# Keys and values of the first attention layer as seven products of quarters instead of eight blocks

## The chip, the cores and the metric

The kernel runs on one core of one Trainium2 chip. The metric is the device time of one execution in microseconds; lower is better. Four runs of the kernel before took 1992.8 to 1999.78 us, with a median of 1995.32 us. All arithmetic is in 32-bit floats.

## What is computed

Two layers follow one another on x, 32 sequences of 64 tokens with 512 features (2048 rows), each with cross attention to a context of the same shape and a feed-forward part:

```python
x = x + L0_xattn(_layernorm(x), ctx, Wq, bq, Wkv, bkv, Wo, bo)
x = x + L0_ffn(_layernorm(x), ...)
x = x + L1_xattn(_layernorm(x), ctx, ...)
x = x + L1_ffn(_layernorm(x), ...)
```

The change lies in the first line, whose core is

```python
q = (query @ Wq + bq).reshape(B, L, NKV, G, HDIM)       # 8 groups of 4 heads of 128
k_, v_ = jnp.split(kv @ Wkv + bkv, 2, axis=-1)          # 8 key heads, 8 value heads
scores = jnp.einsum('blkgd,bmkd->bkglm', q, k) * scale  # within a sequence of 64
attn = jax.nn.softmax(scores, axis=-1)
o = jnp.einsum('bkglm,bmkd->blkgd', attn, v).reshape(B, L, NHEAD * HDIM)
return o @ Wo + bo
```

So for each of 8 groups there is one key head and one value head of 128 features, made from 512 context features for all 2048 rows, and shared by four query heads.

## The kernel before

The 2048 rows are cut into four chunks of 512 rows (eight sequences). Weights and activations lie in SBUF, products go to PSUM, and the language's scheduler orders the instructions of each engine by their dependences; matmuls that are wrapped in `pin` keep the order in which the program writes them. So the order of TensorE (PE) in this layer is written out by hand, and the orders of VectorE (DVE), ScalarE (ACT), GpSimd (POOL) and the DMA queue of SyncE (SP) follow from the scheduler.

**The order of the work.** `order` lists 32 pairs of a chunk c and a group g: the chunks 0 and 1 by turns for all eight groups, then the chunks 2 and 3. One pair is one iteration; two iterations with the same g are one visit, which shares the weights of that group. An iteration i does, in PE's order:

1. the transposes of the softmax result of iteration i-1 (`attn0_turn`, L554, tile pt_o),
2. the query products of iteration i (`attn0_queries`, tiles pqx, pqy, pqz, pqv), between them the mix of the values of iteration i-1 (`attn0_mix`, tile po) and the first of its output products (`attn0_out`, tiles ppx, ppy, ppz),
3. the scores of iteration i (`attn0_scores`, tile sc), 
4. the last three output products of iteration i-1,
5. the keys and values of iteration i+1 (`attn0_keys`, tile pk, and `attn0_values`, tile pv).

The softmax (L365 to L372: maximum, difference, exponential on ScalarE, sum, reciprocal, product) runs on DVE and ScalarE while PE does steps 4 and 5, and is wanted by step 1 of the next iteration.

**Keys and values before.** `attn0_keys` multiplies the weights (512 x 128) with the transposed context (512 x 512) in four matmuls of 512 columns, and ScalarE adds the bias on the way to SBUF (L469). `attn0_values` multiplies the other way round, so that tokens stand on the partitions: four blocks of 128 tokens, four matmuls of 128 columns each, then one DVE copy (L480). In the profile each matmul of 32-bit floats is two instructions, each with a weight load of its own (PEld).

**Strassen's scheme, already used.** The query and output products are made of quarters. Of both operands (512 x 512) the kernel forms sums of quarters: `left_sums` and `right_sums` (L398 to L401 and L408 to L411) are four additions or subtractions each, one of them in place. Seven products of quarters then give the result in place of eight (in Winograd's form, with partial sums that are shared). The products that are shared collect in one PSUM bank x: the first product is copied out by ScalarE (u1), the second is added to the same bank and copied again (u2), then the third (u3). The others go to banks y, z and v, and DVE adds the copies to them (`close`, L502). So PE must wait with the second product on x until the first copy has read it, and with the second product on z until DVE has read z. `quarter` (L426) issues one such product: four matmuls of 256 columns for a 256 x 256 quarter with a contraction of 256.

**Where the sums are made.** The sums of the rows of a chunk are made on DVE by `attn0_in` (with the normalisation L445 and transposes L452); those of the query weights by POOL in `open_visit`, at the end of each odd iteration; those of the output weights by POOL after the scores of each even iteration. POOL also adds the output bias to x (L448).

**Loads.** `load_attn0` loads the weights of a group into one of two slots of the tile `weights`: keys (L121), values (L123), queries (L124), output (L125). `load_ctx` (L186) loads a chunk of the transposed context into `ctx_q`. `clear_list` (L287) fills 4 MB of DRAM with zeros every four iterations; the scheduler places these early. All are issued on SP's queue, in order, each waiting for its place to be free.

**Buffers.** The pool `work` holds four tiles of 128 x 2048 (`t8`: queries and mixed values), three of 128 x 1024 (`t4`: probabilities and their transposes) and seven of 128 x 512 (`t2`: copies, keys, values, normalised rows). PSUM has eight banks: four `mm`, two `tr` (for the x of each scheme), two `sc`.

After the layer, `fold_latent` multiplies two weights of the feed-forward part (tiles pt_fc, pf) between the last output products, and `ffn_in` (L703 to L713) normalises and transposes the first chunk.

Of the kernel before, what the change touches and what calls it, by code (L numbers as in the profile page):

```python
# [12 lines left out]
ALU = mybir.AluOpType  # L13
# [16 lines left out]
def layers(ctx: ExitStack, tc: tile.TileContext, a: dict, out: bass.AP):  # L30
# [5 lines left out]
    xpool = ctx.enter_context(tc.tile_pool(name="xres", bufs=1))  # L36
    work = ctx.enter_context(tc.tile_pool(name="work", bufs=2))
    small = ctx.enter_context(tc.tile_pool(name="small", bufs=4))
    banks = ExitStack()
    pools = {"psum": banks.enter_context(tc.tile_pool(name="psum", bufs=2, space=PSUM))}  # L40
    dram = ctx.enter_context(tc.tile_pool(name="dram", bufs=1, space=bass.MemoryType.DRAM))


# [4 lines left out]
    def quarters(at, n):  # L48
# [3 lines left out]
    rows_q = [quarters(0, 7), quarters(3584, 7)]  # L52
    ctx_q = [
        cells[:, at : at + KT * CH].rearrange("p (k n) -> p k n", k=KT) for at in (7168, 9216)
    ]
    wq_sums, wo_sums, o_sums = (quarters(at, 3) for at in (11264, 12800, 14336))
# [14 lines left out]
    def t8(name):  # L71
        return work.tile([P, 4, 512], F32, tag="t8", name=name, bufs=4)

    def t4(name):
        return work.tile([P, 2, 512], F32, tag="t4", name=name, bufs=3)

    def t2(name):
        return work.tile([P, 512], F32, tag="t2", name=name, bufs=7)

# [18 lines left out]
    def pin(ins):  # L98
        return tc.keep_in_program_order(ins)
# [11 lines left out]
    def rows(ap):  # L111
        return ap.rearrange("(k p) n -> p k n", p=P)

    def part(w, at, k, n):
        return w[:, at : at + k * n].rearrange("p (k n) -> p k n", k=k)

    def load_attn0(g, slot, between=lambda: None):
        w = weights[:, slot]
        wq, wk = part(w, 0, KT, 512), part(w, 2048, KT, P)
        wv, wo = part(w, 2560, KT, P), part(w, 3072, 4, HID)  # L120
        nc.sync.dma_start(wk, rows(a["Wkv"][:, g * P : (g + 1) * P]))  # L121
        between()
        nc.sync.dma_start(wv, rows(a["Wkv"][:, (NG + g) * P : (NG + g + 1) * P]))  # L123
        nc.sync.dma_start(wq, rows(a["Wq"][:, g * 512 : (g + 1) * 512]))  # L124
        nc.sync.dma_start(wo, rows(a["Wo"][g * 512 : (g + 1) * 512, :]))  # L125
        return wq, wk, wv, wo

# [57 lines left out]
    def load_ctx(c, dst):  # L185
        nc.sync.dma_start(dst, rows(a["ctxT"][:, c * CH : (c + 1) * CH]))  # L186

    for c in range(NC):
        for i in range(c * TT, (c + 1) * TT):
            nc.sync.dma_start(xs[i], a["x"][i * P : (i + 1) * P, :])  # L190
        if c == 0:
            w_next = load_attn0(0, 0, between=lambda: load_ctx(0, ctx_q[0]))
        if c == 1:
            load_ctx(c, ctx_q[c])

# [199 lines left out]
    def left_sums(engine, a11, a12, a21, a22, sums):  # L395

        s1, s2, s4 = (sums[:, i] for i in range(3))
        engine.tensor_tensor(s1, a21, a22, ALU.add)  # L398
        engine.tensor_tensor(s2, s1, a11, ALU.subtract)
        engine.tensor_tensor(a21, a11, a21, ALU.subtract)  # L400
        engine.tensor_tensor(s4, a12, s2, ALU.subtract)  # L401
        return {"11": a11, "12": a12, "22": a22, "1": s1, "2": s2, "3": a21, "4": s4}
# [59 lines left out]

    def attn0_keys(g, c, w):
        n = f"a{g}_{c}"
        pk = ps_mm(f"pk_{n}")
        ct = ctx_q[c % 2]
        accumulate_next(pk, [(w[1][:, k, :], ct[:, k, :]) for k in range(KT)])
        kT = t2(f"kT_{n}")
        nc.scalar.activation(kT, pk, AF.Identity, bias=bkv[:, g : g + 1])  # L469
        return kT  # L470

    def attn0_values(g, c, w):
        n = f"a{g}_{c}"
        pv = ps_mm(f"pv_{n}")
        ct = ctx_q[c % 2]
        for t in range(TT):
            s = slice(t * P, (t + 1) * P)
            accumulate_next(pv[:, s], [(ct[:, k, s], w[2][:, k, :]) for k in range(KT)])
        v = t2(f"v_{n}")
        nc.vector.tensor_copy(v, pv)  # L480
        return v

# [51 lines left out]

    def attn0_scores(g, c, kT, qT):
        n = f"a{g}_{c}"
        at = t4(f"at_{n}")
        for p in range(2):
            sc = ps_sc(f"sc_{n}_{p}")
            for b in range(8):  # L540
                s = slice(b * 64, (b + 1) * 64)
                accumulate_next(sc[:, s], [(q_pair(qT, p, b), kT[:, s])])
            softmax(at[:, p, :], sc, 1.0 / math.sqrt(128), f"{n}_{p}")
        return at

    def attn0_turn(g, c, at):
        n = f"o{g}_{c}"

        atT = work.tile([P, TT, 2, P], F32, tag="t4", name=f"atT_{n}", bufs=3)
        for p in range(2):  # L550
            pt = ps_mm(f"pt_{n}_{p}").rearrange("p (t n) -> p t n", t=TT)
            for t in range(TT):
                pin(
                    nc.tensor.transpose(pt[:, t, :], at[:, p, t * P : (t + 1) * P], ident)  # L554
                )
            nc.scalar.copy(atT[:, :, p, :], pt)
        return atT

    def attn0_mix(g, c, v, atT):
        n = f"o{g}_{c}"  # L560

        oT = t8(f"oT_{n}").rearrange("p i (h n) -> p i h n", h=2)
# [55 lines left out]
    def open_visit(v):  # L618
# [3 lines left out]
        visits[v] = {"w": w, "q": left_sums(nc.gpsimd, k11, k21, k12, k22, wq_sums)}  # L622

    rights = {0: attn0_in(0)}
    open_visit(0)
    visits[0]["o"] = right_sums(nc.gpsimd, *w_quarters(visits[0]["w"][3]), wo_sums)
    w = visits[0]["w"]
    kT, v = attn0_keys(0, 0, w), attn0_values(0, 0, w)
    last = None
    for i in range(len(order) + 1):  # L630
        q = iter(())
# [4 lines left out]
        if last is not None:  # L636
            gl, cl, vl, atl = last
            atT = attn0_turn(gl, cl, atl)
        next(q, None), next(q, None)
        if last is not None:  # L640
            o = attn0_out(gl, cl, attn0_mix(gl, cl, vl, atT), visits[(i - 1) // 2]["o"])
        else:
            o = iter(())
# [6 lines left out]
        if i < len(order):  # L650
            at = attn0_scores(g, c, kT, qT)
            last = (g, c, v, at)
        else:
            fold_latent(latent)
# [4 lines left out]
        if i % 2 == 0:  # L659
            if i > 0:  # L660
                visit["o"] = right_sums(nc.gpsimd, *w_quarters(visit["w"][3]), wo_sums)
            if i // 2 + 1 < len(visits):
# [14 lines left out]
        if i + 1 < len(order):  # L677
            cn, gn = order[i + 1]
            if cn not in rights:
                rights[cn] = attn0_in(cn)  # L680
            w = visits[(i + 1) // 2]["w"]
            kT, v = attn0_keys(gn, cn, w), attn0_values(gn, cn, w)
            if gn == NG - 1 and cn + 2 < NC:
                load_ctx(cn + 2, ctx_q[cn % 2])
    down, fc2 = load_down()
# [4 lines left out]
    for c in range(2):  # L690
        load_ctx(c, ctxT[c])


# [862 lines left out]
```

## Time and profile before

| what | value |
|---|---|
| median of four runs | 1995.32 us (1992.8 to 1999.78) |
| profiled execution, whole | 1991.96 us |
| its span, first to last instruction | 1990.1 us |
| granted clock of PE, mean | 0.986 |
| first attention, about | 15 to 1242 us |
| one iteration of it | 37.80 us |
| loads of Wkv | 32 of 256 KB, 2.7 us from issue to landing |

The profile is one execution on the chip. In its groups a line names the place in the code, the engine, the operation, the tile written and the tiles read, the shape, the count, and after the bar the busy time in us, the mean duration of one in ns, and the idle time of the engine just before, with what ended it. PE is the matrix engine, PEld its weight loads, which run beside it; the ends of matmuls are modelled, so that neighbours in a stream overlap by some tenths of a microsecond, and their pitch is read from start to start. In a timeline a row is a start, a length, an engine, a line and an operation; neighbours of one kind are merged (x8).

### The profile page before, as it was taken

The page shows a single profiled execution, that of the slowest core. Times are in us where ns is not written, and L with a number is a line of the kernel's source. Part 1 is how long each engine was busy: PE and PEld are TensorE (multiplying, and loading weights), DVE is VectorE, ACT ScalarE, POOL GpSimd, SP SyncE. Part 2 cuts the span into 40 slices and gives each one's busy share as a digit, 9 for nine tenths or more (in the row PEclk, how much of TensorE's full clock was granted, in tenths as well). Part 3 has the DMA queues.
Part 4 walks back from the last instruction along what each step waited for, and adds up shares of the span by engine and source line. Part 5 has one row for each costly group of instructions (what it writes and reads, how often), then busy time and mean ns, then how long its engine had stood idle before and what let it go on. Part 6 is the DMA issues. An engine that isn't in the chain of part 4 may idle for free.

```text
span 1990.1 us, 26205 instructions
## 1 busy us (share of the span) xinstructions
PE 1908.9 (96%) x10492; PEld 1523.8 (77%) x10492; DVE 1020.6 (51%) x1999; ACT 487.2 (24%) x921; POOL 475.6 (24%) x501
## 2 busy tenths in 40 slices
PE   6999999999999999999999999999999999979993
PEld 5888888888888888888888888687778776655441
DVE  8445345344456644544534545455466466773515
ACT  1211211121121221121112112311221565542221
POOL 5120111111112111211211220141444535540105
PEclk9999999999999999999999999999999999989997
DMA  9993110100120110110100011100003201124628
GB/s 323 275 301 111 44 42 12 54 33 22 57 70 22 54 32 22 54 32 22 54 32 22 22 50 61 55 1 12 0 22 138 65 12 54 70 85 132 217 91 274
DMA packets 136087, 151.69 MB, mean 76 GB/s; under 512 B 4768, under 2 KB 88544, under 8 KB 135968
## 3 DMA queue, kind: packets, MB, share of 16 engines
q1 hardware_dynamic: 124960, 122.70, 19.6%
q0 software_dynamic: 5392, 17.11, 2.6%
q10 hardware_dynamic: 5616, 10.23, 1.4%
q8 instruction: 84, 1.38, 0.3%
q14 instruction: 35, 0.29, 0.1%
HBM read 92.60 MB, written 56.36 MB: 75 GB/s over the span
## 4 chain that ended last, share of the span: by engine, by line
PE 89%; DVE 6%; ACT 2%; DMA 2%; POOL 1%; issue 1%; POOLq 0%; SPq 0%; DVEq 0%; ACTq 0%
PE ppx_o L426 11%; PE pqx_a L426 8%; PE py L105 6%; PE sc_a L105 6%; PE pqz_a L426 6%; PE pv_a L105 6%; PE ppz_o L426 6%; PE pk_a L105 5%; PE po_o L105 3%; PE pdx_f L426 3%; PE ppy_o L426 3%; PE pp L105 3%; PE pqv_a L426 3%; PE pqy_a L426 3%; PE phx_f L426 2%; PE pq_b L105 1%
## 5 line engine op out<-in xcount | busy, mean ns | idle before, releaser
L408 POOL TENSOR_TENSOR arena<-weights 128x512 f32<-128x512 f32 x16 | 20.3, 1268 | 563.0 <-PE ppz_o L426 563.0
L367 ACT ACTIVATE at_a<-at_a 128x512 f32<-128x512 f32 x64 | 40.4, 631 | 444.0 <-DVE at_a L366 444.0
L105 PE MATMUL py<-arena,xT 128*128 x312 | 140.6, 593 | 0.2 <-ACT xT L1272 0.2
L105 PEld LDWEIGHTS pv_a<-weights,arena 128*128 128x128 f32 x1024 | 119.4, 192 | 15.3 <-issue 15.3
L426 PE MATMUL pqz_a<-arena 128*128 128x256 f32 x512 | 122.9, 383 | 4.8 <-DVE qT_a L502 4.8
L426 PE MATMUL ppx_o<-weights,oT_o 128*128 128x256 f32 x512 | 122.8, 383 | 0.1
L105 PEld LDWEIGHTS sc_a<-kT_a,qT_a 128*128 128x128 f32 x1024 | 120.0, 193 | 1.8
L426 PE MATMUL pqx_a<-arena,weights 128*128 128x256 f32 x512 | 121.1, 379 | 0.0
L495 ACT ACTIVATE u_a<-pqx_a,bq 128x256 f32<-128x256 f32 x192 | 80.5, 470 | 163.2 <-PE pqx_a L426 163.2
L105 PE MATMUL pv_a<-weights,arena 128*128 128x128 f32 x1024 | 119.5, 275 | 0.0
L105 PE MATMUL sc_a<-kT_a,qT_a 128*128 128x64 f32 x1024 | 118.3, 274 | 0.0
L105 PE MATMUL pk_a<-arena,weights 128*128 128x512 f32 x256 | 115.1, 592 | 0.0
L480 DVE COPY v_a<-pv_a 128x512 f32<-128x512 f32 x32 | 22.2, 692 | 178.0 <-PE pv_a L105 177.9
L426 PEld LDWEIGHTS pqz_a<-arena 128*128 128x128 f32 x512 | 98.4, 192 | 18.6 <-issue 5.1
L586 DVE TENSOR_TENSOR x<-ppx_o,x 128x512 f32<-128x512 f32 x128 | 86.9, 679 | 45.6 <-PE ppx_o L426 43.8
L426 PEld LDWEIGHTS ppx_o<-weights,oT_o 128*128 128x128 f32 x512 | 94.9, 190 | 11.9 <-ACT oT_o L576 0.5
L426 PEld LDWEIGHTS pqx_a<-arena,weights 128*128 128x128 f32 x512 | 94.9, 190 | 11.5
L502 DVE TENSOR_TENSOR qT_a<-pqz_a,u_a 128x512 f32<-128x512 f32 x64 | 44.2, 691 | 112.2 <-ACT u_a L495 80.2
L105 PEld LDWEIGHTS py<-arena,xT 128*128 128x128 f32 x312 | 56.2, 190 | 55.9 <-issue 55.3
L105 PEld LDWEIGHTS pk_a<-arena,weights 128*128 128x128 f32 x256 | 48.4, 190 | 47.3 <-issue 45.9
L398 POOL TENSOR_TENSOR arena<-weights 128x512 f32<-128x512 f32 x18 | 23.2, 1289 | 245.2 <-PE pqz_a L426 242.2
L502 DVE TENSOR_TENSOR qT_a<-pqy_a,u_a 128x512 f32<-128x512 f32 x32 | 22.1, 691 | 114.9 <-PE pqy_a L426 114.9
(368 smaller groups left out, 3826.1 us busy)
## 6 DMA issues: line engine op xcount, KB each, us to landing
xg<-zero SPq DMA_DIRECT2D x8, 4096.0 KB, 26.0
weights<-in_Wq SPq DMA_DIRECT2D x16, 1024.0 KB, 5.3
weights<-in_Wo SPq DMA_DIRECT2D x16, 1024.0 KB, 5.2
xr<-xg SPq DMA_DIRECT2D x39, 256.0 KB, 3.4
yg<-y ACTq DMA_DIRECT2D x39, 256.0 KB, 2.6
weights<-in_Wkv SPq DMA_DIRECT2D x32, 256.0 KB, 2.7
arena<-in_ctxT SPq DMA_DIRECT2D x8, 1024.0 KB, 5.2
arena<-in_W_e SPq DMA_DIRECT2D x8, 1024.0 KB, 6.2
```

What stands on the lines that cost most here:

```text
L105: nc.tensor.matmul(ps, lhsT, rhs, start=(i == 0), stop=(i == len(pairs) - 1))
L367: nc.scalar.activation(dst, dst, AF.Exp, scale=scale)
L398: engine.tensor_tensor(s1, a21, a22, ALU.add)
L408: engine.tensor_tensor(t1, b12, b11, ALU.subtract)
L426: nc.tensor.matmul(ps[:, m, :], left[:, k, m * P : (m + 1) * P], right[:, k, :], start=first and m == i == k == 0, stop=i == len(pairs) - ...
L480: nc.vector.tensor_copy(v, pv)
L495: nc.scalar.activation(u[:, m * 256 : (m + 1) * 256], ps[:, m * 256 : (m + 1) * 256], AF.Identity, bias=bq[:, 4 * g + 2 * heads + m : 4 * ...
L502: nc.vector.tensor_tensor(q5[:, heads, :, 4 * half : 4 * half + 4, :], ps.rearrange("p (m b q) -> p m b q", m=2, q=64), u.rearrange("p (m ...
L586: nc.vector.tensor_tensor(dst, ps.rearrange("p (m n) -> p m n", m=2), dst, ALU.add)
```

## The change

In the first attention, keys and values of two neighbouring groups in one chunk are now one product of a 512 x 256 weight with the 512 x 512 context, made of quarters by the seven products of the scheme above. A quarter of the weight is 256 x 128, so a product is two matmuls of 256 columns for keys and four of 128 columns for values. One call makes the keys, or the values, of two groups for one chunk; a period of four iterations has two calls for keys and two for values, one at the end of each iteration, where keys and values of the next iteration stood before. Keys are made half a period (two iterations) ahead of their pair of groups, values at the end of the iteration whose mix first uses them. The first call stands before the loop, two stand in the first iteration, and the last two iterations have none.

POOL makes the sums of quarters for the weights (`kv_left`) and for the context (`ctx_right`, once for each chunk). The weights are loaded for two groups at once, the keys into slot 0 and the values into slot 1 of `weights`; a chunk of the context comes in four loads of a quarter each. Keys and values lie in a tile of five places, given out in turn.

The layer gets a pool of its own, `work0`, with two tiles t8, two t4 and four t2, and with the room for the sums and for keys and values. It is closed after the layer, and the pool `work` with the former counts (4, 3, 7) is opened for the rest.

```diff
-    work = ctx.enter_context(tc.tile_pool(name="work", bufs=2))
+    room = ExitStack()
+    pools["work"] = room.enter_context(tc.tile_pool(name="work0", bufs=2))
+    bufs = {"t8": 2, "t4": 2, "t2": 4}
...
+    def load_kv(g, value):
+        w = part(weights[:, value], 2048, KT, 2 * P)
+        at = (value * NG + g) * P
+        nc.sync.dma_start(w, rows(a["Wkv"][:, at : at + 2 * P]))
+        return w
...
-    def attn0_keys(g, c, w):
...
-        accumulate_next(pk, [(w[1][:, k, :], ct[:, k, :]) for k in range(KT)])
...
-    def attn0_values(g, c, w):
...
+    kv_tiles = pools["work"].tile([P, 5, 512], F32, tag="kv", name="kv", bufs=1)
...
+    def kv_left(w, value):
+        k11, k12, k21, k22 = (
+            w[:, 2 * j : 2 * j + 2, i * P : (i + 1) * P] for i in range(2) for j in range(2)
+        )
+        return left_sums(nc.gpsimd, k11, k12, k21, k22, kv_sums[value])
+    def ctx_right(c):
+        x = ctx_q[c % 2]
+        return right_sums(nc.gpsimd, x[:, 0], x[:, 1], x[:, 2], x[:, 3], ctx_sums[c % 2])
+    def attn0_kv(value, g, c, left, right):
...
+        def product(ps, x, y, first=True):
+            x, y = left[x], right[y]
+            for m in range(2 if value else 1):
+                for k in range(2):
+                    sides = (y[:, k, m * P : (m + 1) * P], x[:, k, :]) if value else (
+                        x[:, k, :], y[:, k, :]
+                    )
...
+        def keep(ps, i, name):
+            u = t2(f"{name}_{n}")[:, 0:256]
+            if value:
+                nc.scalar.copy(u, ps[:, 0:256])
+            else:
+                nc.scalar.activation(
+                    u, ps[:, 0:256], AF.Identity, bias=bkv[:, g + i : g + i + 1]
+                )
+            return u
+        def close(i, half, ps, u):
+            nc.vector.tensor_tensor(
+                dst[i][:, half * 256 : half * 256 + 256], ps[:, 0:256], u, ALU.add
+            )
+        x = ps_tr(f"px_{n}")
+        product(x, "11", "11")
+        u1 = keep(x, 0, "u1")
+        y = ps_mm(f"py_{n}")
+        product(y, "12", "21")
+        close(0, 0, y, u1)
+        product(x, "2", "2", first=False)
+        u2 = keep(x, 0, "u2")
+        z = ps_mm(f"pz_{n}")
+        product(z, "1", "1")
+        product(x, "3", "3", first=False)
+        u3 = keep(x, 1, "u3")
+        close(1, 1, z, u3)
+        y = ps_mm(f"pw_{n}")
+        product(y, "22", "4")
+        close(1, 0, y, u3)
+        product(z, "4", "22", first=False)
+        close(0, 1, z, u2)
...
     rights = {0: attn0_in(0)}
+    kv_lefts = [kv_left(w_k, 0), None]
+    ctx_rights = {0: ctx_right(0)}
+    kv_lefts[1] = kv_left(w_v, 1)
     open_visit(0)
...
-    kT, v = attn0_keys(0, 0, w), attn0_values(0, 0, w)
+    make_kv(0, 0, 0)
...
-            kT, v = attn0_keys(gn, cn, w), attn0_values(gn, cn, w)
...
+        p, step = divmod(i, 4)
+        if i == 0:
+            ctx_rights[1] = ctx_right(1)
+            make_kv(0, 0, 1)
+        if step < 2:
+            make_kv(1, p, step)
+        elif p + 1 < NP:
+            make_kv(0, p + 1, step - 2)
+        cp, gp = kv_chunk(p, step % 2)
+        if step < 2 and gp == NG - 2 and cp + 2 < NC:
+            load_ctx(cp + 2, ctx_q[cp % 2])
+            ctx_rights[cp + 2] = ctx_right(cp + 2)
+        if step == 0 and p + 1 < NP:
+            kv_lefts[0] = kv_left(load_kv(kv_chunk(p + 1, 0)[1], 0), 0)
+        elif step == 1 and p + 1 < NP:
+            kv_lefts[1] = kv_left(load_kv(kv_chunk(p + 1, 0)[1], 1), 1)
...
+    room.close()
+    pools["work"] = ctx.enter_context(tc.tile_pool(name="work", bufs=2))
+    bufs.update({"t8": 4, "t4": 3, "t2": 7})
```

In the prediction the seven products of a call are named p1 to p7 in the order of `attn0_kv`.

## The prediction

> **What bounds the kernel now.** I read the page's first part, then the busy times by stretch, then the timeline of one iteration. The page:
>
> ```profile
> PE 1908.9 (96%) x10492; PEld 1523.8 (77%) x10492; DVE 1020.6 (51%) x1999; ACT 487.2 (24%) x921; POOL 475.6 (24%) x501
> ```
>
> Busy times by stretch (stretch, its length, then PE, PEld, DVE, ACT and POOL busy with instruction counts, granted clock, DMA share and GB/s), two neighbouring iterations of the first attention:
>
> ```profile
> 462.20:500.00 37.80, 37.80 (x210) 32.35 (x209) 17.53 (x29) 6.91 (x13) 3.76 (x3) 1.00 0.01 1
> 500.00:537.80 37.80, 37.80 (x210) 32.34 (x209) 17.53 (x29) 6.91 (x13) 6.29 (x5) 1.00 0.21 70
> ```
>
> PE never rests at full clock; every other engine is below half. So from about 50 to 1190 us time falls one for one with PE work, unless the new order makes PE wait. The timeline (start, length, engine, line, operation) shows what is replaced and when DVE is free there:
>
> ```profile
> 537.21 0.69 DVE L372 TENSOR_TENSOR at_a<-at_a,rs_a 128x512 f32<-128x512 f32 x1
> ...
> 537.76 3.60 PE L105 MATMUL pk_a<-arena,weights 128*128 128x512 f32 x8
> 537.96 0.69 DVE L586 TENSOR_TENSOR x<-ppx_o,x 128x512 f32<-128x512 f32 x1
> ...
> 541.19 3.73 PE L105 MATMUL pv_a<-weights,arena 128*128 128x128 f32 x32
> ...
> 544.76 0.49 PE L554 MATMUL pt_o<-ident,at_a 128*128 128x128 f32 x3
> ```
>
> From the first key matmul to the transposes is 544.76 - 537.76 = 7.00 us, 32 times in the layer. DVE has finished the softmax at 537.90 and its last old addition at 538.65.
>
> **1. PE work removed.** After: 32 calls, 16 for the keys and 16 for the values of two groups in a chunk, each seven products. A key product is two matmuls of 256 columns. The same shape stands in the query products: eight instructions 1.73 us apart (513.36 is a stalled one; 515.19 to 516.92), 0.216 each, two per matmul. So 4 x 0.216 = 0.865 us a product, 6.05 a call. A value product is four matmuls of 128 columns, eight instructions at 3.57/32 = 0.11 or, by the weight loads, 0.108: 0.87 to 0.89 us, 6.07 to 6.25 a call. Against 7.00 that saves 0.95 and about 0.90; I take 0.94 x 32 = **30.1 us**. Bounds 27 to 31.
>
> **2. Waits added inside a call.** Order on PE: p1 into x, p2 into y, p3 again into x, p4 into z, p5 into x, p6 into a new bank, p7 again into z. p3 and p5 need ScalarE to have copied x; p7 needs ScalarE's copy after p5 and then the DVE sum that reads z. Before, the same scheme in the queries had 1.73 us of cover a product and no such pause; here it is 0.865. The durations of shapes that exist:
>
> ```profile
> L495 ACT ACTIVATE u_a<-pqx_a,bq 128x256 f32<-128x256 f32 x192 | 80.5, 470 | 163.2 <-PE pqx_a L426 163.2
> ...
> L154 ACT COPY weights<-pf 128x256 f32<-128x256 f32 x4 | 1.5, 372 | 1.8 <-PE pf L96 1.8
> ...
> L1014 DVE TENSOR_TENSOR x<-pp,x 128x256 f32<-128x256 f32 x32 | 13.5, 423 | 66.6 <-PE pp L105 66.6
> ```
>
> Handovers, from the timeline: PE's shown end to ScalarE 0.04 (509.72 to 509.76), ScalarE to DVE 0.03 (519.69 to 519.72), either to PE's weight load 0.05 (1246.01 to 1246.07). A group's shown end is its last start plus 0.38; a group of eight that starts after a wait takes 2.00 instead of 1.89, so 0.11 more.
> - p3, p5 (keys): from the start of p1, its end is at 0.65 + 0.38 = 1.03, the copy ends at 1.03 + 0.04 + 0.47 = 1.54, PE may load at 1.59; its matmul is due at 1.73. Cost about 0.
> - p7 (keys): from p5's start 1.03 + 0.04 + 0.47 + 0.03 + 0.42 + 0.05 = 2.04, due at 1.73: 0.31 + 0.11 = 0.42 us.
> - p7 (values): the copy has no bias, 0.37: 1.94, so 0.21 + 0.11 = 0.32 us.
>
> Together 16 x 0.42 + 16 x 0.32 = **11.8 us**. No row shows PE held by this chain, so both ends: 0 (ScalarE and DVE faster than the shown ends), and 0.8 us a call or 26 us (p3, p5 also late by 0.2 each). I take the chain, as each link has a row. DVE serves it at once: its last queued addition ends 1.1 us into the call, the sum is wanted at about 5.0. ScalarE's last exponential ends at 535.3. Behind p7 stand the transposes, and everything waits with them.
>
> The Trainium skill, "Perfetto Trace Analysis", Optimizing Scalar/DVE Operations, speaks against cutting such work small: it gives about 125 ns of access overhead for a DVE operation on PSUM, about twice that as shown latency. By it the sum of 256 columns would be some 0.27 + 0.25 = 0.52 us, an estimate from that page, and the wait 0.1 us longer in each call, 3 us in all; the row's 423 ns decides here.
>
> **3. Other engines.** DVE gets 128 sums of 0.423 and loses 32 copies of 0.69 (+32 us, on 17.5 of 37.8 busy): hidden. ScalarE gets 96 copies of 0.37 to 0.47 and loses 32 of 0.69: hidden but for step 2. POOL gets 64 sums of 128x256 (row L996, 0.734) and 16 of 128x512 (1.27): 67 us, about 2 in an iteration. They stand behind the query sums and ahead of the output sums on its queue, half a period before use: hidden in the steady part. SP: the built order has Wq, Wkv, Wo and again Wq, Wkv, Wo in each period, each Wkv waiting for a call that ends before the Wo behind it is free, and both are used over one iteration later; 16 loads of 512 KB take the place of 32 of 256 KB (2.7 us to landing). The quarter loads of the context add 12 issues of about 0.4 us. No cost. The buffers cut (t8, t4 and t2 to 2, 2, 4) turn over once in an iteration, each freed before its next writer by the built order: no cost; without that cover PE would wait for one more copy or sum, 0.6 to 0.7 us an iteration.
>
> **4. Start.** Here POOL is on the path. Two engines' sums slow each other, and a rest costs clock:
>
> ```profile
> 16.47 1.71 POOL L398 TENSOR_TENSOR arena<-weights 128x512 f32<-128x512 f32 x1
> ...
> 17.09 1.64 DVE L409 TENSOR_TENSOR arena<-arena 128x512 f32<-128x512 f32 x1
> ...
> 36.18 0.68 DVE L502 TENSOR_TENSOR qT_a<-pqz_a,u_a 128x512 f32<-128x512 f32 x1
> ...
> 36.98 3.06 PEld L426 LDWEIGHTS pqz_a<-arena 128*128 128x128 f32 x8 [5.14 <-issue]
> 37.01 3.75 PE L426 MATMUL pqz_a<-arena 128*128 128x256 f32 x8 [4.77 <-DVE qT_a L502]
> ```
>
> Now POOL makes, after 16.47, four key sums (0.95 each beside DVE) and two context sums (1.7, 1.3) before p3: about 23.3, where PE would be at 16.4. p4 to p7 follow the last two sums (25.9) and, by the 3.75 against 1.89 above, run at half rate at first: the call ends near 29 or 30, against 21.6. The queries then meet the DVE queue, which before held PE until 37.0; with the four sums and their waits in it, it lets go near 42. **+5 us**; bounds +2 (only the DVE queue shifts) and +9 (both add).
>
> The skill's "SBUF — State Buffer", Who interferes with whom, says that DVE and GpSimd operations reading two SBUF inputs exclude each other for a whole instruction. By that the two would take turns, 1.27 + 0.69 = 1.96 us each; the rows show 1.71 and 1.64, and the estimated difference over five sums is about 1 us.
>
> **5. Ends.** The last two iterations have no call: the transposes follow the products at 537.55, the softmax is ready at 537.90: +0.4. The FFN's pool can be written only when the layer's own is given up: its normalised rows, before made in DVE gaps at 1200 to 1210, come after the last addition (ends 1243.35), four of about 0.53; the last feature copy moves from 1246.0 to 1246.7. Together **+1 us**, bounds 0 and 4 (if a load waits too: fc1 now leaves at 1222.4, is wanted at 1229, 256 KB land in 2.7 and 1 MB in 5.3).
>
> **Sum.** -30.1 + 11.8 + 5 + 1 = -12.3 us. The profiled execution took 1991.96 (span 1990.1): 1979.7. The median of the runs is 3.4 above it: **1983**. About 6 us (0.3%) is what a measurement of this kernel can tell from no change.
>
> **Rivals.**
> - *The wait at p7 hardly shows* (chain under cover): -30.1 + 2 + 5 + 1 = -22, 1973. For it: ends of PE are modelled. Against: each link has a row. 0.12.
> - *Waits eat the gain*: 0.7 us a call, 22 us: -30 + 22 + 6 = -2, 1993. For: 0.14 us of slack at p3 and p5. Within 0.3%. 0.17.
> - *Slower*: a product of 0.865 us is no cover at all, p3, p5 and p7 each wait, 1.35 us a call, 43 us: -30 + 43 + 6 = +19, 2014. It decides from (30 - 6)/32 = 0.75 us a call. For: three re-entries in 6 us. Against: each link would have to be 0.3 us longer than its row. 0.09. That the seven products save nothing would end near there; the even pitch of 0.216 and 0.108 speaks against it.
>
> **How the numbers follow.** Forecast 0.62 (own range 1976 to 1989), and all of it and the first rival count as faster: 0.74; within 0.3%: 0.17; slower: 0.09. The range, 1970 to 1994, holds the forecast, most of the first rival and the second at its likeliest time.
>
> **What would show it.** An iteration of 37.2 to 37.3 us instead of 37.80; PE idle before p7 alone, ended by DVE, 0.2 to 0.4 us; a call of 6.4 us; PE's first scores 4 to 6 us later than 40.56. An idle before p3 and p5 or a pitch above 0.216 would make it wrong.

## The result: no faster, about 3 us longer

| | before | after |
|---|---|---|
| median | 1994.67 us (59 runs) | 1997.47 us (36 runs) |
| profiled execution, its span | 1991.96, 1990.1 us | 1995.63, 1993.9 us |

The ratio is 1.0016, with a 95% interval of 1.0009 to 1.0022: 2 to 4 us longer, which is within 0.3%. Forecast were 12.3 us less.

In the page of the kernel after, PE has 15.5 us less work than the 1908.9 before, and yet the span is 3.8 us longer; so PE waits 19 us more.

```profile
PE 1893.4 (95%) x10556; PEld 1542.8 (77%) x10556; DVE 1061.5 (53%) x2095; ACT 505.8 (25%) x985; POOL 546.0 (27%) x581
```

**The steady part does gain.** Busy times by stretch of the kernel after, an iteration that ends in a call for keys and one that ends in a call for values:

```profile
469.55:506.91 37.36, 37.14 (x197) 32.29 (x196) 18.45 (x31) 7.65 (x15) 2.84 (x4) 1.00 0.05 15
506.91:544.31 37.40, 37.32 (x225) 33.56 (x224) 18.54 (x31) 7.35 (x15) 15.11 (x12) 1.00 0.27 85
```

37.36 and 37.40 instead of 37.80; forecast were 37.2 to 37.3. PE is now idle 0.22 and 0.08 us in them. One call for keys in the timeline, p1 to p7 from 440.94 on:

```profile
440.94 1.03 PE L520 MATMUL px_k<-arena,weights 128*128 128x256 f32 x4
441.81 1.03 PE L520 MATMUL py_k<-arena,weights 128*128 128x256 f32 x4
442.67 1.03 PE L520 MATMUL px_k<-kv_room 128*128 128x256 f32 x4
443.53 1.03 PE L520 MATMUL pz_k<-kv_room 128*128 128x256 f32 x4
...
444.39 1.06 PE L520 MATMUL px_k<-arena,weights 128*128 128x256 f32 x4
...
445.29 1.03 PE L520 MATMUL pw_k<-kv_room,weights 128*128 128x256 f32 x4
445.55 0.47 ACT L531 ACTIVATE u_k<-px_k,bkv 128x256 f32<-128x256 f32 x1 [1.28 <-PE px_k L520]
446.05 0.42 DVE L537 TENSOR_TENSOR kv<-pz_k,u_k 128x256 f32<-128x256 f32 x1 [2.69 <-ACT u_k L531]
...
446.53 1.13 PE L520 MATMUL pz_k<-arena,kv_room 128*128 128x256 f32 x4 [0.22 <-DVE kv L537]
...
447.50 1.04 PE L639 MATMUL pt_o<-ident,at_a 128*128 128x128 f32 x8
```

The first six stand 0.86 to 0.90 apart; then p7 waits for the chain that the prediction named: p5's end, ScalarE's copy at 445.55, DVE's sum at 446.05, p7 at 446.53. At the pitch of its neighbours, 0.86, it would have started at 446.15. The call takes 6.56 us instead of 7.00.

**The start eats it.** The start of the first scores (those of iteration 0), of the second (iteration 1) and of later ones splits the span:

| stretch | before | after | difference |
|---|---|---|---|
| start to scores of iteration 0 | 40.56 | 53.82 | +13.26 |
| to scores of iteration 1 (after: one call more, 7.83) | 34.80 | 41.93 | +7.13 |
| to scores of iteration 30 (29 iterations) | 1099.81 | 1087.89 | -11.92 |
| to scores of iteration 31 (after: no call) | 37.81 | 30.80 | -7.01 |
| to the first matmul pe_f of the feed-forward part | 34.09 | 35.14 | +1.05 |
| to the end | 743.03 | 744.32 | +1.29 |

PE at the start, in the timeline of the kernel after:

```profile
23.75 2.08 PE L520 MATMUL px_k<-kv_room 128*128 128x256 f32 x4 [5.94 <-POOL kv_room L425]
...
38.70 1.89 PE L442 MATMUL pqv_a<-arena,weights 128*128 128x256 f32 x8
50.28 3.75 PE L442 MATMUL pqz_a<-arena 128*128 128x256 f32 x8 [9.68 <-DVE qT_a L585]
53.82 3.88 PE L106 MATMUL sc_a<-kv,qT_a 128*128 128x64 f32 x32
```

The first wait is the forecast one: p3 at 23.75 (forecast 23.3), queries from 30.07 (29 to 30). The second was forecast to end near 42 and ends at 50.28. What it waits for stands in the timeline of POOL and DVE:

```profile
28.62 0.42 DVE L537 TENSOR_TENSOR kv<-pz_k,u_k 128x256 f32<-128x256 f32 x1 [6.48 <-ACT u_k L531]
...
31.97 0.62 DVE L373 TENSOR_SCALAR v_a<-mv_a 128x4 f32<-128x4 f32 x1
...
33.73 1.31 DVE L350 TENSOR_SCALAR hf_a<-v_a 128x4 f32<-128x4 f32 x1
33.74 1.27 POOL L424 TENSOR_TENSOR arena<-weights 128x512 f32<-128x512 f32 x1
...
36.41 1.19 DVE L355 SCALAR_TENSOR_TENSOR rs_a<-nw_a,rs_a 128x4 f32<-128x4 f32 x1
37.63 1.19 DVE L353 TENSOR_TENSOR nw_a<-rs_a 128x4 f32<-128x4 f32 x1
...
42.59 0.68 DVE L585 TENSOR_TENSOR qT_a<-pqy_a,u_a 128x512 f32<-128x512 f32 x1
...
49.45 0.68 DVE L585 TENSOR_TENSOR qT_a<-pqz_a,u_a 128x512 f32<-128x512 f32 x1
```

In the kernel before, the same chain; POOL's sums end at 28.24, and from then on it is idle:

```profile
25.78 1.26 DVE L357 TENSOR_SCALAR v_a<-mv_a 128x4 f32<-128x4 f32 x1
27.08 1.19 DVE L330 TENSOR_SCALAR rs_a<-v_a 128x4 int32<-128x4 int32 x1
28.18 0.16 DVE L334 TENSOR_SCALAR hf_a<-v_a 128x4 f32<-128x4 f32 x1
...
28.69 0.16 DVE L339 SCALAR_TENSOR_TENSOR rs_a<-nw_a,rs_a 128x4 f32<-128x4 f32 x1
28.89 0.16 DVE L337 TENSOR_TENSOR nw_a<-rs_a 128x4 f32<-128x4 f32 x1
...
29.96 0.69 DVE L502 TENSOR_TENSOR qT_a<-pqy_a,u_a 128x512 f32<-128x512 f32 x1
```

These are the twelve operations on four numbers a partition that make the reciprocal root for the normalisation of chunk 1. Before, the last ten of them took 0.16 us each. After, POOL sums without a break until 43.88, and eight of the twelve take 1.14 to 1.31 us: as long as one POOL operation (1.27). The closes of the first queries (L585) stand behind them in DVE's queue, and PE behind the closes.

These rows split the 13.26 us by which the first scores are late. The chain starts 6.2 us later (31.97 instead of 25.78): ahead of it DVE stands idle for 6.48 us until a close of the first key call can run, which waits for the copy of p5 and so for p3. From its start to the first query close the chain takes 10.62 us instead of 4.18, 6.4 more. From there to the close that PE waits for (36.18 before, 49.45 after) it is 0.6 more.

### The profile page after: what moved, and what is told of

Read it like the earlier page. It is cut to its first block, busy times and chain, and to the rows that moved or that the text cites. A ratio compares the mean times of both kernels' runs of the same rounds, so it can differ in the third digit from the quotient of the medians.

```text
span 1993.9 us, 26636 instructions
## 1 busy us (share of the span) xinstructions
PE 1893.4 (95%) x10556; PEld 1542.8 (77%) x10556; DVE 1061.5 (53%) x2095; ACT 505.8 (25%) x985; POOL 546.0 (27%) x581
## 4 chain that ended last, share of the span: by engine, by line
PE 87%; DVE 6%; ACT 2%; DMA 2%; issue 1%; POOL 1%; SPq 1%; POOLq 0%; ACTq 0%; DVEq 0%
PE ppx_o L442 11%; PE pqx_a L442 8%; PE py L106 6%; PE sc_a L106 6%; PE pqz_a L442 6%; PE ppz_o L442 6%; PE po_o L106 3%; PE pp L106 3%; PE pdx_f L442 3%; PE ppy_o L442 3%; PE pqv_a L442 3%; PE pqy_a L442 3%; PE px_v L520 2%; PE phx_f L442 2%; PE px_k L520 2%; PE pz_v L520 2%
## 5 line engine op out<-in xcount | busy, mean ns | idle before, releaser
L106 PEld LDWEIGHTS sc_a<-kv,qT_a 128*128 128x128 f32 x1024 | 119.7, 192 | 1.8
L106 PE MATMUL sc_a<-kv,qT_a 128*128 128x64 f32 x1024 | 118.0, 273 | 0.0
L442 PEld LDWEIGHTS pqz_a<-arena 128*128 128x128 f32 x512 | 98.3, 192 | 23.6 <-issue 10.1
L585 DVE TENSOR_TENSOR qT_a<-pqz_a,u_a 128x512 f32<-128x512 f32 x64 | 44.3, 692 | 111.0 <-ACT u_a L578 77.9
L585 DVE TENSOR_TENSOR qT_a<-pqy_a,u_a 128x512 f32<-128x512 f32 x32 | 22.1, 691 | 121.4 <-PE pqy_a L442 121.4
L414 POOL TENSOR_TENSOR kv_room<-weights 128x256 f32<-128x256 f32 x16 | 12.1, 759 | 256.0 <-DMA weights<-in_Wkv 232.2
L1404 DVE TENSOR_TENSOR y<-py,weights 128x512 f32<-128x512 f32 x39 | 26.9, 691 | 85.2 <-PE py L106 80.3
L381 DVE TENSOR_REDUCE mx_a<-sc_a 128x8 f32<-128x512 f32 x64 | 44.3, 692 | 44.5 <-PE sc_a L106 44.5
L106 PE MATMUL po_o<-atT_o,kv 64*128 64x256 f32 x512 | 65.9, 392 | 0.8 <-ACT atT_o L641 0.8
L953 POOL TENSOR_TENSOR s_f<-s_f,arena 128x512 f32<-128x512 f32 x16 | 21.4, 1357 | 157.0 <-DVE s_f L950 117.1
```

The costliest lines, as they stand in the source:

```text
L106: nc.tensor.matmul(ps, lhsT, rhs, start=(i == 0), stop=(i == len(pairs) - 1))
L381: nc.vector.tensor_reduce(mx, p3, AX.X, ALU.max)
L442: nc.tensor.matmul(ps[:, m, :], left[:, k, m * P : (m + 1) * P], right[:, k, :], start=first and m == i == k == 0, stop=i == len(pairs) - ...
L585: nc.vector.tensor_tensor(q5[:, heads, :, 4 * half : 4 * half + 4, :], ps.rearrange("p (m b q) -> p m b q", m=2, q=64), u.rearrange("p (m ...
L953: nc.gpsimd.tensor_tensor(y, y, gamma, ALU.mult)
L1404: pin(nc.vector.tensor_tensor(y, py, be1[:, bass.ds(v[1], 1), :], ALU.add))
```

## Experiments

**Theory**: the sums on POOL slow DVE's small operations, and through DVE's queue they hold PE; the steady gain is real and is cut by the wait at p7. **Rival A**: the start costs only p3's wait and the half clock behind it. **Rival B**: only the new closes in DVE's queue cost. Each run was made beside the kernel before on the same chip; ratios are to that kernel. Where a gain or loss against the kernel after is given in us, it is the difference of the two ratios; that of the kernel after is 1.0016.

### 1. The kernel before with more work for POOL

```diff
+    spare = cells[:, 15872:16384]
+    for _ in range(9):
+        pin(nc.gpsimd.tensor_tensor(spare, ctx_q[1][:, 0], ctx_q[1][:, 1], ALU.add))
     last = None
```

> The kernel before, with nine more additions of 128x512 on POOL behind its eight sums at the start; they write a place that nothing reads, so only POOL's time and its company with DVE change. Theory (POOL's sums slow DVE's small operations): POOL works until about 40 us instead of 28.2, the eleven 128x4 operations of chunk 1's reciprocal root take about 1.2 us each instead of 0.16, the first query close leaves DVE near 38 instead of 29.96, PE's first scores start near 48 instead of 40.56, and the time is 7 to 9 us longer (about 2003). Rival A (the start lost its time only in p3's wait for its sums and the half clock behind it) and rival B (only the new entries in DVE's queue): nothing here waits for these additions and DVE's queue is the same, so 0, within 2 us.

Measured: 2006.34 us beside 1998.62, ratio 1.0036 (1.0022 to 1.0050), 4 to 10 us longer. First scores at 46.55, second at 85.32 instead of 75.36. POOL, DVE and PE in its timeline:

```profile
28.42 12.04 POOL L631 TENSOR_TENSOR arena<-arena 128x512 f32<-128x512 f32 x9
...
28.53 1.18 DVE L337 TENSOR_TENSOR nw_a<-rs_a 128x4 f32<-128x4 f32 x1
29.74 0.16 DVE L338 TENSOR_TENSOR nw_a<-nw_a,hf_a 128x4 f32<-128x4 f32 x1
...
35.03 0.68 DVE L502 TENSOR_TENSOR qT_a<-pqy_a,u_a 128x512 f32<-128x512 f32 x1
...
43.01 3.75 PE L426 MATMUL pqz_a<-arena 128*128 128x256 f32 x8 [10.36 <-DVE qT_a L502]
```

Nobody waits for these nine additions, and DVE's queue has the same order, so A and B fall as the whole cause. The size was off: only every other operation of the chain was slow, so the first close left at 35.03, not 38, and the scores came 6.0 us late, not 7 or 8. The second scores are 10 us late, because PE's clock came back later too. A control in run 6 has such a late clock without more work for POOL (last section), so only the 6.0 us are shown to be POOL's.

### 2. The kernel after with eight sums moved away from the start

```diff
-    visits[0]["o"] = right_sums(nc.gpsimd, *w_quarters(visits[0]["w"][1]), wo_sums)
...
-            ctx_rights[1] = ctx_right(1)
+            with tc.issue_after(biased[-1]):
+                ctx_rights[1] = ctx_right(1)
+                visits[0]["o"] = right_sums(
+                    nc.gpsimd, *w_quarters(visits[0]["w"][1]), wo_sums
+                )
```

(`biased` holds the bias additions of a chunk, L464; `issue_after` puts what it holds behind one instruction in the queue of that engine.)

> The kernel after, with the sums of the first output weights and the context sums of chunk 1 (eight POOL operations of 1.27 us) queued behind the bias additions of chunk 1. p3's operands come as before. Theory: POOL rests from about 33.7, so only the first two or three operations of the root's chain are slow; the first query close comes near 35 instead of 42.6, the seventh query product near 42 instead of 50.28, first scores near 46 instead of 53.82, time 7 to 9 us shorter (about 1989). Rival A (p3's wait): p3 still starts at 23.75, so nothing, within 2 us. Rival B (DVE's queue order): the order is the same, so nothing.

Measured: 2000.27 beside 1998.62, ratio 1.0004 (0.9995 to 1.0013): some 2 us below the kernel after, with intervals that overlap, and not 7 to 9. Its timeline shows both halves of the answer:

```profile
33.37 0.16 DVE L353 TENSOR_TENSOR nw_a<-rs_a 128x4 f32<-128x4 f32 x1
...
34.82 0.69 DVE L587 TENSOR_TENSOR qT_a<-pqy_a,u_a 128x512 f32<-128x512 f32 x1
...
41.95 1.96 PE L442 MATMUL pqz_a<-arena 128*128 128x256 f32 x8 [1.74 <-DVE qT_a L587]
...
55.42 3.31 DVE L388 TENSOR_TENSOR at_a<-at_a,rs_a 128x512 f32<-128x512 f32 x2
...
61.86 2.08 PE L522 MATMUL pz_k<-arena,kv_room 128*128 128x256 f32 x4 [4.16 <-DVE kv L539]
```

With POOL resting from 33.1 the chain takes 0.16 an operation, and the first scores come at 43.75, 10 us earlier: more than forecast. But the eight sums now run at 47.8 to 58.2, beside the first softmax, whose two products take 3.31 us together instead of 1.28; the closes of the next call wait behind them, PE stops 4.16 us before p7 and its clock halves. The second scores come at 94.26, 1.5 us before 95.75. The theory's mechanism holds; that the gain would be kept was wrong.

### 3. Bias additions behind the sums

```diff
-            nc.gpsimd.tensor_tensor(x, x, bo, ALU.add)
+            if c > 0:
+                nc.gpsimd.tensor_tensor(x, x, bo, ALU.add)
...
+    for x in xs[0:TT]:
+        pin(nc.gpsimd.tensor_tensor(x, x, bo, ALU.add))
     make_kv(0, 0, 0)
```

> The kernel after, with the four bias additions of chunk 0 (5.5 us of POOL, 11.2 to 16.7) queued behind the sums of the start, so that the sums begin when their operands land. p3 should start near 18 instead of 23.75 and DVE's idle time of 6.5 us before the second key close should go. Theory: the statistics of chunk 1 then start near 22, but POOL works beside the whole chain, which stays slow (1.2 us an operation), until about 36; scores near 47 to 48, time 5 to 7 us shorter. Rival A (p3's wait and the half clock are the whole cost): the start goes back to within 2 us of the kernel before, scores at 42 or 43, time 11 to 12 us shorter.

Measured: 1997.69 beside 1998.62, ratio 0.9995 (0.9986 to 1.0004), about 4 us below the kernel after. p3 starts at 19.21 and the queries at 24.42, 5.65 earlier; but PE still waits 9.96 us before the seventh query product, with nine of the chain's operations at 1.1 to 1.3, and the first scores come at 48.48, not 42 or 43. Rival A has its 5 us, and no more.

### 4. The seventh product later, twice

```diff
         close(1, 0, y, u3)
+        yield
         product(z, "4", "22", first=False)
...
             atT = attn0_turn(gl, cl, atl)
+        end_kv()
```

> The kernel after, with the seventh product of each call and its close put behind the eight transposes of the next iteration's turn (0.87 us of PE), so that ScalarE's third copy and the DVE sum on bank z have that much more time. Theory (the call loses 0.52 us for keys and 0.35 for values, nearly all of it before p7): no idle time of PE before p7, iterations of 36.9 to 37.0 us instead of 37.36 to 37.40, time 10 to 14 us shorter (about 1985). Rival (the wait is not p7's own but the hand-over's, and comes back at the query product that follows, or the products' pitch is longer than 0.865 and 0.893): iterations of 37.2 to 37.4, time 0 to 5 us shorter.

Measured: 2057.78 beside 1998.62, ratio 1.0302 (1.0288 to 1.0316). In this version the new loads and sums for the next calls came ahead of p7, which multiplied them instead of its own; one iteration in four waited for them, up to 49.0 us long, and most others took 36.87 to 37.06. A second version puts these loads and sums behind `end_kv()`:

```diff
+        for again in reloads:
+            again()
+        reloads.clear()
...
-            kv_lefts[1] = kv_left(load_kv(kv_chunk(p + 1, 0)[1], 1), 1)
+            reloads.append(partial(new_kv, p + 1, 1))
```

> The kernel after, with the seventh product of each call and its close put behind the eight transposes of the next iteration's turn, and the new loads and sums for the next calls behind that product (in the earlier try they came ahead of it, so PE waited for a new load once in four iterations, and p7 read the wrong sums). Theory (a call loses 0.35 to 0.52 us, nearly all before p7): no iteration has the long wait, iterations of 36.9 to 37.1 us instead of 37.36 and 37.40, time 10 to 14 us shorter than the kernel after. Rival (the wait comes back at the product that follows, or the later loads are late): iterations of 37.2 to 37.4, time 0 to 5 us shorter.

Measured: 1986.75 beside 1994.54, ratio 0.9964 (0.9951 to 0.9978), some 10 us below the kernel after. By stretch and in the timeline:

```profile
429.76:466.63 36.87, 36.87 (x197) 32.40 (x196) 18.44 (x31) 7.64 (x15) 10.06 (x8) 1.00 0.18 58
503.50:540.55 37.05, 37.05 (x225) 33.50 (x224) 18.73 (x31) 7.34 (x15) 15.10 (x12) 1.00 0.28 86
```

```profile
442.86 1.03 PE L521 MATMUL pw_k<-kv_room,weights 128*128 128x256 f32 x4
443.72 1.04 PE L641 MATMUL pt_o<-ident,at_a 128*128 128x128 f32 x8
444.59 1.03 PE L521 MATMUL pz_k<-arena,kv_room 128*128 128x256 f32 x4
```

PE is busy for the whole of both iterations: no wait is left, and none came back elsewhere. So 0.49 us (37.36 - 36.87) for keys and 0.35 (37.40 - 37.05) for values were the price of the waits, and seven products without them save 37.80 - 36.87 = 0.93 and 37.80 - 37.05 = 0.75.

### 5. Another order at the start

```diff
-            if cn not in rights:
-                rights[cn] = attn0_in(cn)
+            if cn not in rights and i > 0:
+                with tc.issue_after(closes[3]):
+                    rights[cn] = attn0_in(cn)
...
             make_kv(1, p, step)
...
+        if i == 0:
+            with tc.issue_after(closes[3]):
+                rights[1] = attn0_in(1)
```

(`closes` holds the sums of L585 in order; `closes[3]` is the last one of the first queries.)

> The kernel after with another order at the start and the same work: the statistics and normalised rows of chunks 1 to 3 stand behind the four closes of the first queries in DVE's queue, and on PE the transposes of chunk 1 stand behind the second and third call. POOL's sums are as they were. Theory (the closes wait in DVE's queue behind small operations that POOL slows): the seventh query product follows the sixth near 40.5 instead of 50.28, first scores near 42 instead of 53.82, second scores 7 to 10 us earlier than 95.75, time 6 to 10 us shorter. Rival (POOL's sums hold PE itself, by their operands or memory, not DVE's queue): the sums run as before to 43.9, so scores near 50 or later, time within 3 us.

> The order of the run above and the bias additions of chunk 0 behind the sums of the start, so that both stalls of the start are taken away. p3 was found at 19.2 with the bias additions late, so the queries should start near 24.5, first scores near 37 and second scores 11 to 14 us before 95.75: time 10 to 14 us shorter than the kernel after, so 8 to 11 below the kernel before. If the two stalls are one and the same (the second only moves when the first goes), the gain is that of the run above, 6 to 10.

> Both edits of the start and the later seventh product together. If start and steady part are separate terms of the sum, the gains add: 10 to 14 for the start and 10 to 14 for p7, 20 to 28 us below the kernel after, near 1975 where the kernel before takes 1995. If the later p7 only shifts the wait to what follows, 10 to 16.

Measured beside 1994.54: the order alone 1994.76, ratio 1.0000 (0.9992 to 1.0009); with the bias additions of chunk 0 late 1987.09, 0.9961 (0.9947 to 0.9975); with the later p7 as well 1973.73, 0.9894 (0.9876 to 0.9911). The timeline of the order alone:

```profile
39.66 1.89 PE L442 MATMUL pqv_a<-arena,weights 128*128 128x256 f32 x8
41.62 1.96 PE L442 MATMUL pqz_a<-arena 128*128 128x256 f32 x8
43.42 3.84 PE L106 MATMUL sc_a<-kv,qT_a 128*128 128x64 f32 x32
...
62.96 1.64 PE L468 MATMUL pt_a<-ident,h_a 128*128 128x128 f32 x8 [2.28 <-DVE h_a L461]
...
75.79 1.13 PE L106 MATMUL po_o<-atT_o,kv 64*128 64x256 f32 x6 [3.07 <-DVE qT_a L587]
```

POOL sums as long as in the kernel after, to 43.7, and PE does not stop before the seventh query product: there the sums hold PE through DVE's queue and through nothing else, and the rival "POOL holds PE itself" falls. (Before p3 PE still waits 6.30 us for a sum that it multiplies.) Again most is lost in iteration 0, where the rows and the small operations of chunk 1 now meet POOL's bias additions (four rows 3.27 us), and PE stops for 2.28 and 3.07: second scores at 94.18, a gain of 1.6 instead of the expected 7 to 10, and the time is some 3 us below the kernel after, not 6 to 10. With the bias additions of chunk 0 late too they come at 85.33, 10.4 us earlier, a little less than the expected 11 to 14; the time is some 11 us below. All three edits: scores of iteration 31 at 1192.72, 21.7 us before the kernel after, against 10.1 and 10.8 for the two parts alone. So start and steady part are separate terms, and this version is 1.06% faster than the kernel before (0.89 to 1.24).

### 6. Bias additions out of the start, and two controls

The first takes the bias additions of chunks 0 and 1 out of the start in the fastest version and puts them into iterations 1 and 2; the second gives the start edits of run 5 to the kernel before; the third only closes the kernel before's pool ahead of the feed-forward part and opens one of the same size.

```diff
+        if i in (1, 2):
+            for x in xs[(i - 1) * TT : i * TT]:
+                nc.gpsimd.tensor_tensor(x, x, bo, ALU.add)
```

> The fastest version so far (order of the start, later seventh product), with the bias additions of chunks 0 and 1 (eight POOL operations, 10.2 us) taken out of the start and added to the same rows after their first output products. In the version before it (first scores 36.73, second 86.42), iteration 0 lost about 8 us to DVE operations beside these additions (rows of chunk 1 3.8 us for four instead of about 2, small operations at 0.7 to 1.2). Theory (POOL beside DVE's SBUF operations): second scores 2 to 5 us earlier than 86.42, iterations unchanged at 36.87 and 37.05, time 2 to 5 us below 1973.7 where the kernel before takes 1994.5. Rival (iteration 0 lost its time to the new order of PE and DVE alone): nothing, within 1.5 us.

> The kernel before, with the same two edits of the start (order of DVE and PE, bias additions of chunk 0 behind the sums), to see what of their gain belongs to the change. There PE idles 5.1 us before the seventh query product and works at a lower clock after it. If that idle time is what the edits take, first scores near 34 instead of 40.56, and as in the changed kernel some of it is lost again in iteration 0: time 2 to 6 us shorter. If POOL's longer queue is what made the start bad, the gain here is small, 0 to 2 us, against about 10 in the changed kernel.

> The kernel before, with the layer's pool closed and one of the same size opened ahead of the feed-forward part, and nothing else. Theory: the normalised rows of the first chunk of that part, made by DVE at 1200 to 1210, move behind the last addition to x, at about 1244; PE waits about 1.3 us there and the end of the span moves by 1 to 2.5 us; the first attention keeps its times. Rival (the tail's loss has another cause): rows stay near 1205, difference under 0.5 us in the profile's times at 1240 to 1290.

Measured beside 1994.42: 1975.62, ratio 0.9898 (0.9882 to 0.9915), not to be told from the version before it, where 2 to 5 us less were expected; in the profile the second scores do come at 83.71, 2.7 us earlier. The kernel before with the edited start: 1998.67, 1.0018 (1.0008 to 1.0028), 2 to 6 us longer instead of shorter. Its first scores come at 35.12, as expected, but PE then stops 6.25 us before the transposes of chunk 1, and the second scores come at 79.96 instead of 75.36. So the gain of these edits belongs to the changed kernel; the kernel before has nothing of it. The pool alone: 1997.04, 1.0007 (0.9996 to 1.0018), no difference that can be told; its timeline shows the step at the boundary:

```profile
1246.29 0.69 DVE L587 TENSOR_TENSOR x<-ppx_o,x 128x512 f32<-128x512 f32 x1 [1.04 <-PE ppx_o L427]
1246.90 1.90 DVE L707 TENSOR_SCALAR h_f<-x,mv_f,rs_f 128x512 f32<-128x512 f32 x4
...
1247.58 1.06 PE L713 MATMUL pt_f<-ident,h_f 128*128 128x128 f32 x8 [1.33 <-DVE h_f L707]
```

All four rows now come behind the last addition. From the scores of iteration 31 to pe_f it takes 35.14 us (1216.61 to 1251.75) instead of 34.09: the +1.05 of the changed kernel, exactly. "The first attention keeps its times" was wrong by 3.6 us in iteration 0, by the clock alone (last section).

## Why the prediction was wrong

The terms of its sum, with what they measured:

| step | predicted | measured | from |
|---|---|---|---|
| 1. work removed | -30.1 | -26.9 | run 4: 16 x 0.93 + 16 x 0.75 |
| 2. waits in a call | +11.8 | +13.4 | run 4: 16 x 0.49 + 16 x 0.35 |
| 4. start | +5 | about +15 | what is left of the span's +3.8 |
| 5. ends | +1 | +1.05 | pool control; the last two iterations cost nothing (30.80 = 37.81 - 7.01) |
| unassigned, after pe_f | 0 | +1.29 | |
| sum | -12.3 | +3.8 | |

**Step 4 failed**: "+5 us; bounds +2 (only the DVE queue shifts) and +9 (both add)". Its first half was right to half a microsecond. For the second it said that the queries "meet the DVE queue, which before held PE until 37.0; with the four sums and their waits in it, it lets go near 42". That moved the queue by a few of its own sums and left its other entries at their old durations. That shift was sized well, 5 us for the 6.2 measured. But POOL's queue is sixteen operations longer and reaches to 43.9, and most of the small operations that took 0.16 take about 1.2 beside it: 6.4 us that the sum put at nothing. PE was let go at 50.28, not near 42. Run 1 shows this without any part of the change, runs 2 and 5 show it by taking away either the company or the queue's order.

The rows that warned were in the trace of before: two of these same operations, at 25.8 and 27.1, took 1.26 and 1.19 while POOL still worked, and the next, at 28.18, 0.16. The prediction weighed the rule of the Trainium skill, "SBUF — State Buffer", Who interferes with whom (a DVE operation with two SBUF inputs, or in one of its fast modes, and a GpSimd operation exclude each other for a whole instruction), only on the large sums, where it comes to 1 us. The measured rows agree with the rule where it costs most: a wait of one whole instruction is a seven- or eightfold price for a small operation, though not each one pays it (here 8 of 12, every other one in run 1). They agree, too, in what is spared: statistics (0.66) and closes from PSUM (0.68) kept their times beside POOL.

**Step 1** was mis-sized by 3.2 us. It had worked out 6.07 to 6.25 us for a value call, and took "about 0.90" saved where 7.00 - 6.25 = 0.75 was its own other end; the value products stand 0.893 apart, which gives 6.24 in run 4. Its low bound, 27, is the measured sum.

**Step 2** was right in mechanism and near in size: p7 alone, 0.49 and 0.35 where 0.42 and 0.32 were forecast. DVE's sum took the 0.42 us of its row, not the 0.52 estimated beside it from the skill's page; and that page advises larger operations for an engine that is saturated, which DVE, busy for 18.45 of 37.36 us, was not. **Step 3** (POOL costs nothing in the steady part) holds: run 4 has iterations in which POOL sums 10 and 15 us and PE never rests.

**Step 5** is right for the boundary. The last +1.29 cannot be assigned: from the scores of iteration 31 to the end, the kernel before took 777.1 us in its profiled execution, and the same code 786.8 in run 1 and 781.0 in the first control of run 6, so single executions differ there by more than that.

The rival "Waits eat the gain" gave 1993 and a time within 0.3%, which lies nearest to what came. That was chance: its waits of 22 us were 13.4, and the loss sat in the start.

The 15 us of the start are a remainder, but the stretches give nearly the same: at the second scores the kernel after is 20.39 us late, of which 5.7 are three calls of steady length in place of two pairs of blocks (a key call 6.56, a value call 6.60, a pair of blocks 7.00). That leaves 14.7.

What stays open is how much of the 15 us each part of the start has by itself, beyond the split of the first 13.26: the parts hand time to each other (run 2 and the order alone in run 5 gained 10 us at the first scores and kept 1.5 and 1.6). The best start tried gives back 12.0 of it.

## What to carry to other kernels

Before sums are given to an idle GpSimd, list what DVE does in the same microseconds: its small operations on SBUF can cost up to one GpSimd operation each, and whatever stands behind them in its queue, PSUM closes for PE above all, is late by the sum. In a scheme that enters a PSUM bank again, put a piece of other PE work as long as the copy and the sum between the two products; here 0.87 us of transposes, as long as copy and sum (0.47 + 0.42), was worth 10 us. And a stall taken away at a crowded start comes back at the next crowded place, so read the gain at a later mark, not at the stall.

## What the runs showed of the hardware

The half clock behind a stall cost about 2 us in two kernels and about 6 in two others (an estimate: half of the time from PE's return to work to the full clock, given below). Busy times by stretch, 44 to 56 us, of the kernel before, of the pool control and of run 1 (after the times, the granted clock is the third number from the end):

```profile
44.00:56.00 12.00, 12.00 (x80) 9.88 (x80) 9.39 (x31) 4.84 (x9) 0.00 (x0) 1.00 0.54 161
```

```profile
44.00:56.00 12.00, 12.00 (x65) 10.09 (x65) 9.25 (x31) 3.81 (x7) 0.00 (x0) 0.78 0.47 141
```

```profile
44.00:56.00 12.00, 12.00 (x53) 11.43 (x52) 7.68 (x19) 1.59 (x3) 3.29 (x3) 0.51 0.40 122
```

PE is busy all the time in all three, and does 80, 65 and 53 instructions. Read in stretches of 1 us, the clock is at 0.50 for about 6.8 us in the kernel before, 10.2 in the kernel after, 13.6 in the pool control and 20.5 in run 1. PE went back to work at 37.01, 50.28, 36.75 and 43.01, and the full clock came 4.5, 3.8, 12.5 and 12.8 us later. The pool control and the kernel before have the same start, with stalls of 4.25 and 4.77 us and first scores at 40.29 and 40.56; PE is busy from the return on in both, so the clock alone makes the second scores 3.6 us later (78.93 and 75.36). What decides between a short and a long return is not shown.

The Trainium skill, "TensorE: Matmul & The Clock Gate", Part 1: The HAM clock gate (the "warmup" mystery), has a free-running window of about 3.4 us and a return to full rate after at least one busy window; what is issued behind the first 3.4 us, it says, runs at full rate. The lengths here, two, three, four and six times 3.4, agree with the windows; the return after 12.5 and 12.8 us of work does not agree with a return behind the first 3.4.
